# Two groups of edges in one PSUM bank, evicted together

## The chip, the cores and the metric

The kernel runs on 1 core of one Trainium2 chip. The metric is the device time of one execution in microseconds (us). Five engines run their own instruction streams and meet through semaphores: TensorE (PE; its weight loads are listed apart as PEld), VectorE (DVE), ScalarE (ACT), GpSimd (POOL) and SyncE (SP), which issues most DMAs. PE writes its results to PSUM, which has eight banks; each bank holds 512 float32 columns in each of 128 partitions.

## The reference

Two layers of a graph network on N = 1250 nodes with 1024 features and 41250 edges (`src`, `dst`, sorted by `dst`, each with one of two relations). Cut to what matters here:

```python
h = relu(layernorm(x))
# layer 0: relational convolution, D_FF = 286
norm_x = ln_weight * h * rsqrt(mean(h*h) + 1e-6)
out = norm_x @ W_root + bias
for r in range(2):
    w = (edge_type == r)
    sums = segment_sum((norm_x[src] @ W_rel[r]) * w[:, None], dst)
    out = out + sums / max(segment_sum(w, dst), 1)[:, None]
x = x + h + elu(out) @ wo
# layer 1: graph attention over the same edges
g = relu(layernorm(x)) @ W
e = exp(-leaky_relu(al[src] + ar[dst], 0.1))
x = x + elu(segment_sum(e * g[dst], src) / (segment_sum(e, src) + 1e-5))
```

## The kernel before

Both layers use a dense matrix of counts: how many edges of relation r go from node s to node d. The kernel keeps it in SBUF as the tile `cnt` in fp16. Its rows (the partitions) are the source nodes modulo 128; its columns are 20 blocks (10 source tiles times 2 relations) of 1280 destination nodes. With it the segment sums become matrix products: `means(t)` (L800) multiplies `cnt` with the rows `y`, ten destination tiles one after the other, and starts once all of `cnt` is there.

The change is in the first stage, which builds `cnt` while it computes the products of layer 0. It takes the first 190 us or so. Its two strands are these.

**The products.** For each of 10 node tiles t there are 16 steps, each a matmul of 429 columns in float32 at L723 (eight slices of the 1024 features, two halves). Around them stand, for tiles ahead and behind, by a fixed table (`plan`, `first_plan`, `late_plan`): the row statistics (DVE) and `rstd` (ACT, L550), `norm`, which makes `h` (ACT, L560), `square`, which makes the mean square and `rms` (ACT, L566 and L568), `turn(t, g)`, four PE transposes of `h` into a bank `tp` (L578), `scaled(t, g)`, four ACT copies out of that bank into `hT` (L585), and the three parts that turn the product into `y` (DVE L593, L599, L610, L616; ACT L603, L612). `residual` (POOL, L589) issues the DMA that adds `h` to `x`. `count_over` (DVE, L656 to L661, once, in tile 2) looks for edges that the fast way can't hold.

**The counts.** The edges stand in 162 groups (NG) of 256; a group is two chunks (J) of 128 edges, one edge to a partition. All edges of a group have destinations within W = 12 columns of the group's first one. For each chunk DVE compares a number of the edge with a counter and so makes a one-hot row of 2 x 10 x 12 = 240 columns, `key` (L522; five buffers). For two groups at a time it makes the one-hot rows of the source nodes, `lo` (L495; two buffers). PE multiplies the two (L523), which adds up the counts of the group in 240 columns of a PSUM bank. After the first chunk of a group a matmul of 20 columns (L526) adds what the last chunk before it left over for this group's first column. When the second chunk is in, ACT reads the group's first destination from SBUF into a register (L528) and copies the 240 sums to their place in `cnt` at that offset (L530): 20 blocks of 12 columns. Windows of neighbouring groups overlap, and the later group's copy is the valid one, so the copies must land in the order of the groups.

`chunks()` is a generator, and the loop over the steps draws from it after each L723 matmul about two chunks, spread evenly over the 160 steps. The order on PE, DVE and ACT is the written order of the program; nothing is reordered by a scheduler.

The banks: two pairs hold the products (`mm`). The other four hold the counts and the transposes. `bank(name)` takes one of three, the one freed longest, and `own_bank(name)` a fourth; groups with q % 4 == 3 take the fourth, and the other groups, the two transpose tiles of each node tile and a small one (`turn_worst`) share the three. A matmul that opens a bank waits until ACT has read what was in it.

The lines of a group, as they stand:

```python
acc = (own_bank if q % 4 == 3 else bank)("acc").rearrange("p a b -> p (a b)")
a3 = acc[:, :2 * T * W].rearrange("p (c w) -> p c w", w=W)
...
if j == J - 1:
    b = nc.values_load(first[0:1, q:q + 1], engines=[mybir.EngineType.Activation], ...)
    nc.scalar.activation(cnt_w[:, :, bass.ds(b, W)], a3, AF.Copy)
```

Of the kernel before, what the change touches and what calls it, by code (L numbers as in the profile page):

```python
# [13 lines left out]
AF = mybir.ActivationFunctionType  # L14
# [12 lines left out]
N = 1250  # L27
T = 10
ROWS = [min(128, N - t * 128) for t in range(T)]
PE_ = 128  # L30
J = 2
GE = J * PE_
NG = 162
W = 12
# [376 lines left out]
def fast_arm(tc, ctx, edges, firsts, w_root, conv_bias, wo, w_gat, a_gat, out,  # L411
# [4 lines left out]
    nc = tc.nc  # L416
# [7 lines left out]
    cnt_w = cnt_raw.rearrange("p (c n) -> p c n", n=NPAD)  # L424
# [47 lines left out]
    with ExitStack() as c1:  # L472
# [5 lines left out]
        first = firsts_at[:PE_]  # L478

        idle = own_bank("idle")  # L480
        for _ in range(12):
# [8 lines left out]
            engines={mybir.EngineType.PE, mybir.EngineType.DVE, mybir.EngineType.Activation}))  # L490
        los = {}

        def low_hots(q):
            los[q // 2] = hot.tile([PE_, 128, 2 * J], BF16, name="lo", bufs=2)
            nc.vector.tensor_tensor(  # L495
                los[q // 2], iota_lo,
                lows[:, q:q + 2, :].rearrange("p q j -> p (q j)")[:, None, :].to_broadcast([PE_, 128, 2 * J]),
                ALU.is_equal,
            )

        def carry_hots(q, q1):
            nc.vector.tensor_tensor(hot_ck[:, q:q1], iota_ck[:, None, :].to_broadcast([PE_, q1 - q, 2 * T]),
                                    ck[:, q:q1, None].to_broadcast([PE_, q1 - q, 2 * T]), ALU.is_equal)
# [3 lines left out]
        def chunks():  # L507

            for q in range(NG):
                if q % 2 == 0 and q // 2 not in los:  # L510
                    low_hots(q)
                if q in CARRIES:
                    carry_hots(q, CARRIES[q])
                acc = (own_bank if q % 4 == 3 else bank)("acc").rearrange("p a b -> p (a b)")
                a3 = acc[:, :2 * T * W].rearrange("p (c w) -> p c w", w=W)
                if q:

                    last = los[(q - 1) // 2][:, :, ((q - 1) % 2) * J + J - 1]
                    carry = (a3[:, :, 0:1], last, hot_ck[:, q - 1, :, None])
                for j in range(J):  # L520
                    key = hot.tile([PE_, 2 * T * W], BF16, name="key")
                    nc.vector.tensor_scalar(key, iota_key, keys[:, q, j:j + 1], None, op0=ALU.is_equal)  # L522
                    nc.tensor.matmul(acc[:, :2 * T * W], los[q // 2][:, :, (q % 2) * J + j], key, start=(j == 0),  # L523
                                     stop=(j == J - 1))
                    if q and j == 0:
                        nc.tensor.matmul(*carry, start=False, stop=False)  # L526
                    if j == J - 1:
                        b = nc.values_load(first[0:1, q:q + 1], engines=[mybir.EngineType.Activation],  # L528
                                           min_val=0, max_val=N - 1)
                        nc.scalar.activation(cnt_w[:, :, bass.ds(b, W)], a3, AF.Copy)  # L530
                    yield

        chunk = chunks()

        def some(n):
# [170 lines left out]
        for t in range(T):  # L706
            pys[t] = ps.tile([128, 2, 512], F32, name="mm")
            for i in range(SK):
# [12 lines left out]
                if (t, i) in late_plan:  # L721
                    late_plan[t, i]()
                nc.tensor.matmul(pys[t][:ROWS[t], r, :F + HF], hTs[t][0][:, k, :ROWS[t]], wcat[k][:, r, :],  # L723
                                 start=(k == 0), stop=(k == KD - 1))
# [492 lines left out]
    with tc.manual_schedule(  # L1217
            engines={mybir.EngineType.PE, mybir.EngineType.DVE, mybir.EngineType.Activation}):
# [84 lines left out]
    with tc.manual_schedule(  # L1303
            engines={mybir.EngineType.PE, mybir.EngineType.DVE, mybir.EngineType.Activation,
                     mybir.EngineType.Pool}):
# [264 lines left out]
```

## Time and profile before

| what | before |
|---|---|
| median of 3 executions (lowest to highest) | 593.46 us (593.29 to 594.02) |
| the profiled execution: its time, its span | 593.43 us, 591.6 us |
| PE busy | 571.1 us (97% of the span) |
| DVE busy | 412.0 us (70%) |
| ACT busy | 284.2 us (48%) |
| granted clock of PE, mean | 0.996 |

The span goes from the first to the last instruction. A matmul's end is modelled from how matmuls follow each other in the pipeline, so "busy" includes some overlap; what counts is when the next one starts. In the list of waits a line reads: engine, tile and line that waited, after the arrow what it waited for, then the total in us, how often, and the longest. In the timeline a line reads: start in us, duration, engine, line, operation, output<-inputs, shapes, count, and in brackets the idle time of the engine before it and what ended it. In the busy time by stretches the columns are the busy us of PE, PEld, DVE, ACT and POOL with the number of instructions, the granted clock of PE as a share of full speed, the share of DMA time and GB/s.

### The profile page before, as it was taken

To read this page: it belongs to the slowest core of one execution; us is meant where nothing else is said; L and a number is where in the kernel's file an instruction comes from. 1 tells how busy PE (TensorE), PEld (TensorE's weight loads), DVE (VectorE), ACT (ScalarE), POOL (GpSimd) and SP (SyncE) were. 2 spreads that over 40 slices of the span, in tenths; PEclk is the share of its full clock that TensorE was granted. 3 is DMA by queue.
4 is the path that set the end of the run, shared out by engine and by line. 5 is a ranking of instruction groups with operands and counts; after the bars stand their busy time and mean duration, and the time that the engine had idled before them with its cause. 6 is when DMAs were issued, how large, how long until landed. Compare 5 with 4: busy or idle time off the path is not lost. (4 is left out here: it accounts for less than half of the span.)

```text
span 591.6 us, 8893 instructions
## 1 busy us (share of the span) xinstructions
PE 571.1 (97%) x2894; PEld 412.1 (70%) x2894; DVE 412.0 (70%) x1051; ACT 284.2 (48%) x694; POOL 25.6 (4%) x41
## 2 busy tenths in 40 slices
PE   7899999999999999999999999999999999999994
PEld 5555555655555776776766788888888778888872
DVE  5788787887774666658899926141749988887732
ACT  3676666756663000002332124253727488877722
POOL 4010000000000000000000000000033000000000
PEclk9999999999999999999999999999999999999998
DMA  8951111011105800010015730000010122222211
GB/s 280 342 138 19 37 37 37 13 24 36 29 2 212 248 37 37 35 72 37 37 71 166 209 98 0 2 0 1 0 37 2 37 101 78 75 94 81 86 67 50
DMA packets 21933, 43.85 MB, mean 74 GB/s; under 512 B 2511, under 2 KB 7887, under 8 KB 21877
## 3 DMA queue, kind: packets, MB, share of 16 engines
q1 hardware_dynamic: 20308, 38.07, 18.7%
q0 software_dynamic: 1424, 5.12, 4.6%
q8 instruction: 24, 0.39, 0.3%
q14 instruction: 33, 0.26, 0.2%
q10 hardware_dynamic: 144, 0.00, 0.0%
HBM read 24.55 MB, written 13.52 MB: 64 GB/s over the span
## 5 line engine op out<-in xcount | busy, mean ns | idle before, releaser
L723 PE MATMUL mm<-w,hT 128*128 128x429 f32 (+1 forms) x320 | 145.8, 542 | 1.7 <-DMA w<-in_w_cat_dram 1.7
L530 ACT ACTIVATE cnt<-acc 128x240 f32 x162 | 63.5, 392 | 61.0 <-PE acc L523 38.5
L522 DVE TENSOR_SCALAR key<-meta 128x240 bf16<-128x240 f16 x324 | 74.9, 277 | 4.6 <-PE acc L523 1.8
L800 PE MATMUL mm<-y,cnt 128*128 128x286 bf16 (+3 forms) x600 | 75.2, 285 | 0.3 <-DVE y L616 0.3
L800 PEld LDWEIGHTS <-cnt 128*128 128x128 f16 (+1 forms) x600 | 59.5, 99 | 14.7 <-issue 1.0
L523 PEld LDWEIGHTS <-lo 128*128 128x128 bf16 x324 | 35.7, 114 | 44.4 <-issue 23.7
L523 PE MATMUL acc<-key,lo 128*128 128x240 bf16 x324 | 61.6, 268 | 4.7 <-ACT cnt L530 3.9
L723 PEld LDWEIGHTS mm<-w,hT 128*128 128x128 f32 (+1 forms) x320 | 48.8, 190 | 6.2 <-issue 3.7
L495 DVE TENSOR_TENSOR lo<-meta 128x512 bf16<-128x512 f16 x81 | 34.1, 421 | 26.0 <-PE acc L526 25.1
L991 PE MATMUL mm<-w,a 128*128 128x257 f32 (+3 forms) x192 | 44.5, 379 | 0.0
L811 ACT ACTIVATE bias<-bias 128x286 f32<-128x286 f32 (+1 forms) x10 | 4.4, 442 | 80.2 <-DVE bias L810 80.2
L991 PEld LDWEIGHTS mm<-w,a 128*128 128x128 f32 (+1 forms) x192 | 35.7, 187 | 5.5 <-ACT h L1017 0.2
L846 PE MATMUL mm<-wo,meta 128*128 128x512 f32 (+1 forms) x80 | 37.6, 592 | 0.0
L526 PEld LDWEIGHTS <-lo 128*128 128x128 bf16 x161 | 18.3, 114 | 24.1 <-issue 24.0
L1099 ACT ACTIVATE d<-meta,score 128x128 f32<-128x128 f32 x84 | 27.2, 389 | 10.0 <-DVE d L1116 10.0
L1161 PE MATMUL tp<-hm,zm 128*128 128x512 f32 (+1 forms) x120 | 30.1, 400 | 0.6 <-ACT tp L1167 0.6
L526 PE MATMUL acc<-meta,lo 128*128 128x20 bf16 x161 | 29.4, 183 | 0.0
L1099 ACT ACTIVATE d<-meta,tenths 128x128 f32<-128x128 f32 x84 | 27.2, 389 | 0.0
L1161 PEld LDWEIGHTS tp<-hm,zm 128*128 128x128 f32 (+1 forms) x120 | 21.6, 184 | 6.0 <-ACT tp L1167 0.6
L1161 PE MATMUL tp<-hh,zh 128*128 128x512 f32 (+3 forms) x60 | 23.7, 396 | 0.0
L1161 PE MATMUL tp<-parts,zl 128*128 128x512 f32 (+3 forms) x60 | 23.7, 395 | 0.0
L1161 PE MATMUL tp<-hh,parts 128*128 128x512 f32 (+1 forms) x60 | 23.6, 394 | 0.0
(207 smaller groups left out, 1010.3 us busy)
## 6 DMA issues: line engine op xcount, KB each, us to landing
x<-h POOLq DMA_DIRECT2D x9, 512.0 KB, 5.1
xd<-x SPq DMA_DIRECT2D x9, 512.0 KB, 2.6
x<-in_x_dram SPq DMA_DIRECT2D x8, 512.0 KB, 12.8
w<-in_L_gnn_W_dram SPq DMA_DIRECT2D x8, 512.0 KB, 7.5
w<-in_w_cat_dram SPq DMA_DIRECT2D x8, 429.0 KB, 10.1
squares<-cnt SPq DMA_DIRECT2D x10, 320.0 KB, 3.4
d<-squares SPq DMA_DIRECT2D x40, 80.0 KB, 2.1
d<-xd SPq DMA_DIRECT2D x9, 256.0 KB, 2.8
```

The lines of the kernel that those rows point to most:

```text
L495: nc.vector.tensor_tensor(los[q // 2], iota_lo, lows[:, q:q + 2, :].rearrange("p q j -> p (q j)")[:, None, :].to_broadcast([PE_, 128, 2 * J]),
L522: nc.vector.tensor_scalar(key, iota_key, keys[:, q, j:j + 1], None, op0=ALU.is_equal)
L523: nc.tensor.matmul(acc[:, :2 * T * W], los[q // 2][:, :, (q % 2) * J + j], key, start=(j == 0), stop=(j == J - 1))
L526: nc.tensor.matmul(*carry, start=False, stop=False)
L530: nc.scalar.activation(cnt_w[:, :, bass.ds(b, W)], a3, AF.Copy)
L723: nc.tensor.matmul(pys[t][:ROWS[t], r, :F + HF], hTs[t][0][:, k, :ROWS[t]], wcat[k][:, r, :], start=(k == 0), stop=(k == KD - 1))
L800: nc.tensor.matmul(pm[:n, r, :f], cnt[:k, h, r, t * 128:t * 128 + n], ybs[h][:k, s, r, :f], start=(h == 0 and s == 0), stop=(h == T - 1 an ...
L811: nc.scalar.activation(ex[:n], ex[:n], AF.Exp)
L846: nc.tensor.matmul(po[:n, c, :], oT[:, i, :n], wo_of[i][:, cs], start=(i == 0), stop=False)
L991: nc.tensor.matmul(o[:a.shape[2], :c1 - c0], a[:, k, :], b[k][:, c0:c1], start=(start and k == 0), stop=(k == KH - 1), skip_group_check=no ...
L1099: nc.scalar.activation(form[:, t - t0, :], rows[:, s, :], AF.Exp, bias=n[:, t:t + 1], scale=scale)
L1161: nc.tensor.matmul(sums_of[s, c][:n], at(sets[s % 2][f], t, t + 1)[:k, 0, :n], h[:k, c * HD:c * HD + HD], start=(t == 0 and f == "h"), sto ...
```

## The change

Group q and group q+1 (q even) now share one bank: the first takes its columns 0 to 239, the second 240 to 479. A bank is taken for each even group; every fourth pair (q % 8 == 6) takes the fourth bank. The copies of both groups, with their register loads, are issued behind the second matmul of the odd group, first the even one's, then the odd one's. There are as many matmuls, keys, register loads and copies as before, of the same sizes.

```diff
-                acc = (own_bank if q % 4 == 3 else bank)("acc").rearrange("p a b -> p (a b)")
-                a3 = acc[:, :2 * T * W].rearrange("p (c w) -> p c w", w=W)
+
+                if q % 2 == 0:
+                    both = (own_bank if q % 8 == 6 else bank)("acc").rearrange("p a b -> p (a b)")
+                acc = both[:, q % 2 * 2 * T * W:(q % 2 + 1) * 2 * T * W]
+                a3s = acc.rearrange("p (c w) -> p c w", w=W)
+                reads = [(q, a3s)] if q % 2 == 0 else [reads[0], (q, a3s)]
                 if q:
 
                     last = los[(q - 1) // 2][:, :, ((q - 1) % 2) * J + J - 1]
-                    carry = (a3[:, :, 0:1], last, hot_ck[:, q - 1, :, None])
+                    carry = (a3s[:, :, 0:1], last, hot_ck[:, q - 1, :, None])
                 for j in range(J):
                     key = hot.tile([PE_, 2 * T * W], BF16, name="key")
                     nc.vector.tensor_scalar(key, iota_key, keys[:, q, j:j + 1], None, op0=ALU.is_equal)
-                    nc.tensor.matmul(acc[:, :2 * T * W], los[q // 2][:, :, (q % 2) * J + j], key, start=(j == 0),
+                    nc.tensor.matmul(acc, los[q // 2][:, :, (q % 2) * J + j], key, start=(j == 0),
                                      stop=(j == J - 1))
                     if q and j == 0:
                         nc.tensor.matmul(*carry, start=False, stop=False)
-                    if j == J - 1:
-                        b = nc.values_load(first[0:1, q:q + 1], engines=[mybir.EngineType.Activation],
-                                           min_val=0, max_val=N - 1)
-                        nc.scalar.activation(cnt_w[:, :, bass.ds(b, W)], a3, AF.Copy)
+                    if j == J - 1 and len(reads) == 2:
+                        for g, a3 in reads:
+                            b = nc.values_load(first[0:1, g:g + 1], engines=[mybir.EngineType.Activation],
+                                               min_val=0, max_val=N - 1)
+                            nc.scalar.activation(cnt_w[:, :, bass.ds(b, W)], a3, AF.Copy)
                     yield
```

## The prediction

> **What bounds the kernel now.** I first read the busy time by stretches, to see where PE is not full.
>
> ```profile
> 80.00:100.00 20.00, 19.42 (x104) 11.53 (x103) 15.44 (x60) 13.10 (x38) 1.53 (x3) 1.00 0.14 27
> 200.00:220.00 20.00, 20.00 (x144) 14.68 (x142) 14.18 (x34) 0.89 (x2) 0.00 (x0) 1.00 0.27 83
> ```
>
> Behind the count stage (200 us on) PE is busy for all 20 us of each stretch; in it, some 0.6 us of 20 are lost at full granted clock. ACT has room (13.1 of 20). Whatever PE loses in this stage moves the whole rest, which PE bounds. So next the list of waits, PE's alone:
>
> ```profile
> PE acc L523 <- ACT cnt L530: 3.9, 5, 1.1
> PE mm L723 <- DMA w<-in_w_cat_dram: 1.7, 2, 1.1
> ...
> PE tp L578 <- ACT hT L585: 1.2, 2, 0.6
> PE acc L523 <- ACT hT L585: 0.8, 1, 0.8
> ...
> PE tp L578 <- ACT cnt L530: 0.3, 1, 0.3
> ```
>
> Four of these are one cause: PE opens a PSUM bank whose last contents ACT has not copied out yet, counts (L530) or transposes (L585). That makes 6.2 us; the weights' DMA is early (10.9 and 18.9 us) and not touched. How such a wait looks, in the timelines of PE and of ACT:
>
> ```profile
> 65.12 0.27 PE L523 MATMUL acc<-key,lo 128*128 128x240 bf16 x1
> 66.52 0.27 PE L523 MATMUL acc<-key,lo 128*128 128x240 bf16 x1 [1.12 <-ACT cnt L530]
> 66.62 0.18 PE L526 MATMUL acc<-meta,lo 128*128 128x20 bf16 x1
> ```
>
> ```profile
> 65.37 0.29 ACT L568 ACTIVATE rms<-ssq,eps 128x1 f32<-128x1 f32 x1
> 66.03 0.44 ACT L530 ACTIVATE cnt<-acc 128x240 f32 x1 [0.37 <-issue]
> 66.75 0.44 ACT L530 ACTIVATE cnt<-acc 128x240 f32 x1 [0.29 <-ACT cnt L530]
> 67.47 0.44 ACT L530 ACTIVATE cnt<-acc 128x240 f32 x1 [0.28 <-ACT cnt L530]
> ```
>
> ACT was held up by `sq` and `rms`, copies at 66.03 to 66.47, and PE starts at 66.52. From start to start that step took 1.40 us; where PE doesn't wait it takes 0.10 to 0.11, so the loss is 1.29, more than the idle 1.12 that the bracket shows, as ends are modelled. I summed the losses so, start to start against the median of like steps: 22.7 us 0.23, 25.8 0.94, 38.3 0.57, 42.9 0.06, 45.6 0.64, 47.7 1.07, 61.1 0.14, 66.5 1.29, 94.6 0.73, 103.0 1.00, 130.7 0.73, 138.9 0.71, 156.4 0.21, 164.0 0.26. Together **8.6 us**, all of them waits for a bank. The last two ACT rows show the other price that I need: copies that follow each other come every 0.72 us (the register load on ACT's queue stands between), or about 0.46 where ACT was busy with something long and the load ran ahead (60.63 and 61.09).
>
> **The change, part by part.**
>
> *Banks.* PE and DVE keep the same instructions in the same order, and PE's matmuls have the same sizes: nothing there (loads of weights and keys as before). A bank is now taken per two groups. A group takes some 1.04 us of PE (67.56, 68.59, 69.63, 70.67), so with four banks a bank comes up again after about 8 groups, 8.3 us, instead of 4.2: 4.1 us more. It is held longer by one group and by the second copy, 1.04 + 0.72 = 1.8 us. Net, PE should come about 2.3 us later than ACT's release compared to now. I checked it wait by wait: for each matmul that opens a bank in the changed program I looked up what it waits for, and took both times from this trace. Now there are 157 such waits; in the median PE comes 1.5 us after ACT's instruction has ended, 12 of them under 0.1 us (PE waited), 25 under 0.7. With the new banks there are 81; median 3.5 us, one under 0.1, four under 0.7. The wait at 66.5 is gone altogether (that group is the second of its pair), and the next opening, at 67.56, has 5.0 us to spare, 3.7 once PE comes 1.29 sooner.
>
> *The copies.* As many as before (162 by 392 ns), with as many register loads. Even ones move behind the odd group's second matmul. So what stands behind a pair on ACT (L550, L560, L566, L568, L585, L603, L612) starts up to 0.72 us later wherever ACT had been waiting for PE; where ACT was behind, nothing changes. Who waits for those: PE for L585 and L560, DVE for L550, L568, L603, L612, POOL for `h` (its DMA lands 5 us after the issue and is needed a tile of 17 us later). ACT does wait for PE often (38.5 us in 56 places), so the delay is real; what counts is whether somebody is there. DVE in this stage waits mostly for PE, and for ACT two times, 0.7 us each. PE's openings behind L585 with under 0.72 us to spare are few: at 77.6 us (0.50 us) and 113.8 (0.29), so at worst (0.72 − 0.50) + (0.72 − 0.29) = 0.65; I take 0.53, by a delay of 0.66. SP's and POOL's queues keep their order.
>
> *What is left of the 8.6.* Four places. At 25.8 us the bank still holds transposes; with the 0.94 + 0.23 before it gone PE arrives at the next opening at 26.81 − 1.17 = 25.64, ACT's last `hT` copy ends at 25.79: 0.15. At 38.3 the transposes need the pair of groups 18 and 19, whose copies now follow each other behind `y` (37.30, then 0.30 to 0.46 later): 0.2. At 130.7:
>
> ```profile
> 129.09 0.38 ACT L530 ACTIVATE cnt<-acc 128x240 f32 x1 [0.53 <-PE acc L523]
> 129.35 0.28 ACT L550 ACTIVATE rstd<-mv,eps 128x1 f32<-128x1 f32 x1
> 129.54 1.13 ACT L585 ACTIVATE hT<-tp,lnw 128x128 f32<-128x128 f32 x4
> ```
>
> ```profile
> 129.97 0.18 PE L526 MATMUL acc<-meta,lo 128*128 128x20 bf16 x1
> 130.72 0.66 PE L578 MATMUL tp<-ident,h 128*128 128x128 f32 x4 [0.57 <-ACT hT L585]
> ```
>
> The transposes wait for four `hT` copies that stand behind a group's copy. In the changed program they need the pair 106 and 107 instead: the first copy starts at 129.09, the second 0.66 later and ends at 130.12; PE would be there at 129.99, so 0.16 with the 0.05 of the signal. At 94.6 the copies of `hT` now stand ahead of group 72's copy (92.95) instead of behind it, and the wait is gone. Fourth, what was covered: at 45 to 47 us DVE does `count_over`, and its next key ends at 47.18. Without 0.64 + 1.07 PE is there at 48.67 − 1.71 = 46.96: about 0.3 us, DVE being late next. DVE's keys already cost PE 0.4 us (31.2, 52.8, 79.8, 91.2); with PE closer behind I add as much again.
>
> *The end of the stage.* The last pair's second copy ends at about 184.1 instead of 183.4; `means` reads `cnt` from 187 us on, covered by the last L723 matmuls; 0.7 if they were not there.
>
> Sum: 8.56 − (0.15 + 0.2 + 0.16 + 0.3 + 0.53 + 0.4 = 1.74) = 6.8 us. Against the profiled execution: 593.43 − 6.8 = **586.6 us** (its median stands at 593.46, the same within 0.03).
>
> **The rivals.** *The waits only move* (the burst is paid widely): ACT's delay of 0.7 us behind pairs reaches PE at half of the 18 sets of `hT` copies from tile 1 on: 6.3 us, leaving a gain of 2.3: 591.2 us. For it: ACT waits for PE at 56 places, and a `hT` copy ended four of the waits above. Against it: only two openings have less than 0.7 us to spare.
>
> *Keys.* DVE is busy for 15 to 17 us of 20 in this stage; if it, not ACT, is the next bound, a gain ends where PE has caught up. Its keys are ready 1.17 us ahead in the median, but under 0.6 us in 25 of 324 cases; if those each cost 0.15 us, the gain is 8.56 − 3.75 − 1.34 (the other terms) = 3.5: 590.0. Against it: DVE itself waits 25.1 us for PE to free `lo`, so it follows PE.
>
> *The bank becomes scarcer* (slower): the copy is late by a group, and transposes do not keep the groups' rhythm. If the 18 sets of transposes from tile 1 on found the pair just copied and each waited 0.7 us for its second copy, that is 12.6 us against 8.6 removed: 597.4. It decides once more than 12 of the 18 wait so. Against it: by the banks of the changed program one does (130.7). The Trainium skill, "PSUM — Partial Sum Buffer", section "Summary: rules for kernel authors", speaks against the change in this sense: evacuate promptly, as PSUM is tight; and it has PE and the reader use different banks, which is why the even group's copy must wait at all. By that rule the time would come out as this rival's. This trace does not bear it out: ACT's spare time is the longer one by the 2.3 us above.
>
> *No change:* some later wait takes up the gain, for instance the DMAs of the next stage's weights, which start when the products end. They would have to end last, but PE is full from 200 us on, and the list shows no wait for them. 593.4.
>
> **How the numbers follow.** About 0.2% (1.2 us) is what a measurement of this kernel tells from no change. Forecast 0.64 (584.9 to 589), waits that move or keys 0.21 (589 to 592.2), no change 0.05, scarcer banks or another loss 0.10. So faster 0.85, same 0.05, slower 0.10. Range: from all 8.6 us gained with nothing left, 584.9, to the weakest of the partial cases, 591.2.
>
> **What would show it.** Right: PE's waits for ACT in the first 190 us fall from 6.2 us to under 1.5; none of the long ones at `rms`; ACT's waits at L530's successor come half as often and are longer; the second copy of each pair follows the first by about 0.7 us; means starts some 7 us earlier and the rest of the trace keeps its length. Wrong: PE waits for `hT` or `h` in many places (the burst), PE's weight loads and matmuls wait for `key` (DVE), or the first stage shortens and a later stage grows.

## The result, and the profile after

| | before | changed |
|---|---|---|
| median (lowest to highest), 4 runs each on one chip | 593.59 us (593.29 to 594.02) | 587.16 us (587.08 to 587.84) |
| ratio, 95% interval | | 0.9894 [0.9877, 0.9911] |
| profiled execution: time, span | 593.43, 591.6 us | 587.84, 586.0 us |
| start of the last matmul of the products (L723, now L728) | 186.73 us | 181.18 us |
| from there to the end of the span | 404.9 us | 404.9 us |

The changed kernel is 6.4 us faster. The whole difference lies in the first stage; behind it nothing changed length. From L523 on the lines have moved by 4 or 5: the chunk's matmul is L527, the small one L530, the register load L533, the copy L535, transposes L583, `hT` copies L590.

The busy time by stretches, changed kernel (busy us of PE, PEld, DVE, ACT, POOL; granted clock; DMA):

```profile
80.00:100.00 20.00, 20.00 (x108) 11.96 (x107) 16.04 (x61) 13.43 (x37) 1.28 (x3) 1.00 0.24 46
200.00:220.00 20.00, 20.00 (x122) 13.41 (x121) 13.88 (x34) 0.89 (x2) 0.00 (x0) 1.00 0.07 27
```

The stretch that had 19.42 us of PE is now full. PE's waits, in the order of their totals:

```profile
PE mm L728 <- DMA w<-in_w_cat_dram: 2.7, 2, 2.0
...
PE acc L527 <- ACT hT L590: 1.1, 2, 0.8
```

Of the four kinds of waits for a bank one stands there still, with 1.1 us in two places. The weights' DMA, which the change doesn't touch, is 1.0 us longer than in the profile of before. ACT's own waits from 14 to 190 us, before and then after:

```profile
ACT cnt L530 <- PE acc L523: 38.5, 56, 5.2
ACT cnt L530 <- ACT cnt L530: 10.7, 33, 0.8
```

```profile
ACT cnt L535 <- PE acc L527: 25.2, 32, 7.2
ACT cnt L535 <- ACT cnt L535: 22.3, 74, 0.9
```

By this list ACT waited for PE 38.5 us in 56 places and now does 25.2 us in 32; copy behind copy went from 33 to 74 places. So the copies do come in pairs. The name PE is not right everywhere: in 37 of the 56 places, and in 19 of the 32, the last matmul that the copy needs had ended more than 0.35 us before the copy started, and ACT waited for its own register load. The place of the 1.29 us loss, PE's and then ACT's timeline:

```profile
63.77 0.27 PE L527 MATMUL acc<-key,lo 128*128 128x240 bf16 x1
63.87 0.18 PE L530 MATMUL acc<-meta,lo 128*128 128x20 bf16 x1
63.90 0.38 PE L527 MATMUL acc<-key,lo 128*128 128x240 bf16 x2
```

```profile
63.40 0.29 ACT L573 ACTIVATE rms<-ssq,eps 128x1 f32<-128x1 f32 x1
64.66 0.44 ACT L535 ACTIVATE cnt<-acc 128x240 f32 x1 [0.97 <-PE acc L527]
65.32 0.44 ACT L535 ACTIVATE cnt<-acc 128x240 f32 x1 [0.23 <-ACT cnt L535]
```

The last row of PE merges two matmuls; the second of them, at 64.01 us, is the one that stood at 66.52 before, and it no longer waits. The 0.97 us that ACT stands idle behind `rms` are put down to PE by the bracket, but the last matmul of that pair had ended at 61.3 us. It is the register load, which started at 63.40 and took 0.88 us; PE now has the room to go on meanwhile. The second copy follows the first after 0.66 us.

By the prediction's method (start to start, against the median of like steps) PE's losses to banks fell from 8.6 to 1.9 us: 0.99 at 27.4 us, 0.26 at 38.6, 0.47 at 75.6, 0.18 at 126.4. Losses to late keys rose from 0.37 to 0.73, those to the weights' DMA from 2.1 to 3.1. That is −6.7 + 0.35 + 1.0 = −5.35 us; the last L728 starts 5.55 us sooner, and the two profiled executions are 5.59 us apart. The other three executions of the changed kernel took 587.08 to 587.21.

### The profile page after: what moved, and what is told of

It reads as the page before. It is cut to its first block, busy times and chain, and to the rows that moved or that the text cites. A ratio compares the mean times of both kernels' runs of the same rounds, so it can differ in the third digit from the quotient of the medians.

```text
span 586.0 us, 8877 instructions
## 1 busy us (share of the span) xinstructions
PE 569.8 (97%) x2894; PEld 412.3 (70%) x2894; DVE 411.1 (70%) x1051; ACT 286.7 (49%) x694; POOL 26.3 (4%) x41
## 5 line engine op out<-in xcount | busy, mean ns | idle before, releaser
L728 PE MATMUL mm<-w,hT 128*128 128x429 f32 (+1 forms) x320 | 145.8, 542 | 2.7 <-DMA w<-in_w_cat_dram 2.7
L535 ACT ACTIVATE cnt<-acc 128x240 f32 x162 | 63.5, 392 | 53.7 <-PE acc L527 25.2
L527 PEld LDWEIGHTS <-lo 128*128 128x128 bf16 x324 | 35.7, 113 | 45.3 <-issue 30.6
L527 PE MATMUL acc<-key,lo 128*128 128x240 bf16 x324 | 61.0, 268 | 1.2 <-ACT hT L590 1.1
L728 PEld LDWEIGHTS mm<-w,hT 128*128 128x128 f32 (+1 forms) x320 | 48.7, 189 | 7.2 <-issue 6.4
L530 PEld LDWEIGHTS <-lo 128*128 128x128 bf16 x161 | 18.3, 114 | 19.0 <-issue 18.7
L530 PE MATMUL acc<-meta,lo 128*128 128x20 bf16 x161 | 29.4, 183 | 0.0
```

The source lines that it names most:

```text
L527: nc.tensor.matmul(acc, los[q // 2][:, :, (q % 2) * J + j], key, start=(j == 0), stop=(j == J - 1))
```

## The experiments

The theory: the gain comes from the time until a bank is opened again, which doubles. Rivals: it comes from the copies (they stand elsewhere on ACT's queue, in pairs), or from one bad place that happened to move. Besides the times, I summed PE's losses from 10 to 197 us in each profile (every start that comes over 0.03 us late, against the medians of both kernels), by what the profile names as the releaser:

| kernel | profiled us | banks (ACT) | keys, `lo` (DVE) | weights (DMA) | time less losses |
|---|---|---|---|---|---|
| before | 593.43 | 8.5 | 0.9 | 2.0 | 582.0 |
| changed | 587.84 | 2.0 | 1.1 | 3.0 | 581.7 |
| changed, again | 587.10 | 1.8 | 1.0 | 2.7 | 581.6 |
| copies in pairs only | 593.48 | 8.6 | 0.8 | 2.1 | 582.0 |
| pairs, three banks | 590.39 | 5.6 | 0.75 | 2.3 | 581.7 |
| before, three banks | 601.50 | 15.2 | 1.3 | 2.7 | 582.3 |
| both loads first | 597.88 | 8.6 | 5.4 | 2.0 | 581.9 |
| before, add on POOL | 597.91 | 2.1 | 10.4 | 1.4 | 584.0 |
| eight keys | 586.71 | 1.5 | 1.25 | 2.4 | 581.6 |
| loads first, eight keys | 596.80 | 7.65 | 4.75 | 2.2 | 582.2 |

In all but one the time less the losses is the same within 0.7 us: what PE loses in this stage decides the time. (The DVE column holds a wait of `means` for `y` too, 0.5 us in before and after.)

**The copies alone.** The kernel before, a bank for each group, but both copies behind the odd group:

```diff
-                if q % 2 == 0:
-                    both = (own_bank if q % 8 == 6 else bank)("acc").rearrange("p a b -> p (a b)")
-                acc = both[:, q % 2 * 2 * T * W:(q % 2 + 1) * 2 * T * W]
+                acc = (own_bank if q % 4 == 3 else bank)("acc").rearrange("p a b -> p (a b)")[:, :2 * T * W]
```

(against the changed kernel)

> The copies of two groups stand behind the odd group's second matmul, as in the changed kernel, but each group has a bank of its own, as in the kernel before. Theory (banks): the gain is the longer time until a bank comes up again; here that stays at four groups (4.2 us) while each even group holds its bank for some 1.8 us longer, so nothing is gained and PE waits for banks more than the 8.6 us of before: 594 to 602 us. Rival (ACT's queue): the gain comes from half as many waits of ACT for PE and from copies that follow each other; those are here too, so 587 to 589 us.

593.55 us, ratio to before 0.9993 [0.9983, 1.0002]. Its list of PE's waits (its lines are 2 above those of the changed kernel):

```profile
PE acc L525 <- ACT cnt L533: 2.7, 4, 1.1
...
PE acc L525 <- ACT hT L588: 1.6, 3, 0.6
PE tp L581 <- ACT hT L588: 1.1, 2, 0.6
PE tp L581 <- ACT cnt L533: 0.6, 1, 0.6
```

All four kinds of bank waits of before are back, with 6.0 us by the list (6.2 before). So the pairing of the copies brings nothing. It costs nothing either: I had expected 594 to 602 us, as the even group's bank is held a group longer. But it hardly is: in the median the even group's copy ends 1.4 us behind that group's second matmul in place of 1.2 before, the odd one's 1.0 in place of 1.1. ACT was mostly behind by about a group already.

**Fewer banks.** The same comparison with the fourth bank left empty, once for pairs, once for single groups:

```diff
-                    both = (own_bank if q % 8 == 6 else bank)("acc").rearrange("p a b -> p (a b)")
+                    both = bank("acc").rearrange("p a b -> p (a b)")
```

> The changed kernel with three banks for counts and transposes instead of four (the fourth stands empty). Theory (banks): a bank comes up after six groups, 6.2 us, instead of 8.3; that is 2.1 us more than before, of which the longer hold takes 1.8: most of the gain is gone, 590 to 594 us, with PE's waits for ACT back at 4 to 8 us. Rival (ACT's queue): 587 us, as ACT's instructions are the same.

```diff
-                acc = (own_bank if q % 4 == 3 else bank)("acc").rearrange("p a b -> p (a b)")
+                acc = bank("acc").rearrange("p a b -> p (a b)")
```

> The kernel before with three banks instead of four for counts and transposes: a bank comes up after 3.1 us instead of 4.2. Theory (banks): the openings lose 1.0 us of their room (median 1.5), so a third to a half of the 157 waits bite: 605 to 625 us. Rival (ACT's queue): ACT's instructions are those of before, so about 593 us, at most a few us more.

Pairs on three banks: 590.79 us, ratio 0.9949 [0.9932, 0.9965]. Single groups on three: 601.95 us, 1.014 [1.012, 1.016], less than I had expected. PE's longest waits for banks from 14 to 190 us, the pairs first, then the single groups:

```profile
PE acc L527 <- ACT cnt L535: 2.2, 4, 0.8
PE tp L583 <- ACT cnt L535: 1.1, 3, 0.6
```

```profile
PE acc L523 <- ACT cnt L530: 8.9, 11, 1.6
PE tp L578 <- ACT hT L585: 2.1, 4, 0.6
PE tp L578 <- ACT cnt L530: 1.0, 1, 1.0
```

The four versions lie in order of the time until a bank is opened again (banks times groups in each times the 1.04 us of a group, transposes aside): 3.1 us 601.95, 4.2 us 593.97 (before, on the same chip), 6.2 us 590.79, 8.3 us 587.16 (the result above). The first step gives 8.0 us for 1.04 us more, the other two 3.2 and 3.6 us for 2.08 us each; that fewer of ACT's delays outlast a longer time is the likely reason, but it was not counted. Three shared banks beat four single ones. This is what the theory says and neither rival does. One thing this series doesn't part: from single groups to pairs the times that PE opens a bank also fall, from 183 to 102 in the stage, and on three banks a pair finds its bank free no earlier than a single group did on four (0.9 and 1.1 us before PE comes, in the median). So the 3.2 us of the middle step may be for the fewer openings as much as for the longer time. The other two steps keep the number of openings and show the time alone.

**What makes the copies late.** The big losses before follow a pattern. ACT's queue at the place of the 1.29 us: the register load at 62.62 us took 0.86 us in place of 0.28, so the copy behind it started at 63.91; `sq` and `rms` stood next, and the following load and copy could only start at 65.38 and 66.03. Ten of the stage's register loads took over 0.7 us, and every one of them lies between the issue and the landing of a `residual` DMA (this one 61.0 to 66.1). The loads of the kernel before (shortest/median/longest ns):

```profile
L528 ACTq TENSOR_LOAD <-meta x162: 270/276/1188, 9.7 to 182.1; - x162
```

To see whether that DMA slows them, the addition goes to POOL itself:

```diff
-            nc.gpsimd.dma_start(xs[t][:n], hs_.pop(t)[:n], accum_op=ALU.add)
+            nc.gpsimd.tensor_add(xs[t][:n], xs[t][:n], hs_.pop(t)[:n])
```

> The kernel before, with x + h added by an instruction of POOL instead of by an accumulating DMA (residual). In the trace of before ACT's register loads (L528, 0.28 us) take 0.4 to 1.2 us in the 5 us in which that DMA runs, and the long waits of PE stand behind them. Theory: the DMA slows the loads; without it they stay at 0.28 and the waits at 45.6, 66.5, 103.0 and 138.9 us shrink by some 0.6 each: 590.5 to 591.5 us unless POOL's add slows DVE. Rival: the loads are slow for another reason (they stand behind a blocked queue), stay at 0.9, and the time stays at 593 us or grows.

598.06 us, ratio 1.0072 [1.0055, 1.0088], not the 590.5 to 591.5 us of the theory, which held only if POOL's addition did not slow DVE. The loads of that kernel:

```profile
L528 ACTq TENSOR_LOAD <-meta x162: 271/275/481, 9.8 to 184.9; - x162
```

With the DMA the longest takes 1188 ns, without it none is over 481. That the DMA slows the loads is shown. The losses to banks fell to 2.1 us, but this can't be put down to the loads alone, as PE came later for another reason. POOL's and DVE's timelines:

```profile
62.06 2.35 POOL L589 TENSOR_TENSOR x<-x,h 128x1024 f32<-128x1024 f32 x1 [8.23 <-ACT h L560]
```

```profile
62.69 2.02 DVE L495 TENSOR_TENSOR lo<-meta 128x512 bf16<-128x512 f16 x1 [0.75 <-PE acc L526]
```

`lo`, 0.42 us elsewhere, takes 2.02 and ends 0.3 us behind POOL's addition; a key that meets such an addition takes up to 2.51 us in place of 0.28. The Trainium skill, "SBUF — State Buffer", section "Who interferes with whom", says that a DVE instruction with two SBUF inputs contends with a GpSimd instruction that reads SBUF; the 2.02 us agree. Some 2 us of that kernel's time lie outside the losses counted (584.0 in the table). Of these 1.6 lie behind DVE's last instruction, where the span runs on for 7.8 us in place of 6.2, so not in this stage; why is open. So the DMA is the cheaper of the two, and the sharing of banks makes nearly all its slow loads harmless: in the changed kernel they go on (0.88 us at 63.4 us), and from 39 us on no wait of PE for a bank follows one within 11 us. No kernel was run that has neither the DMA nor POOL's addition.

**Both loads ahead of both copies.** If the 0.66 us of a pair were of weight, loading both offsets first should shorten it:

```diff
-                        for g, a3 in reads:
-                            b = nc.values_load(first[0:1, g:g + 1], ...)
+                        places = [nc.values_load(first[0:1, g:g + 1], ...) for g, _ in reads]
+                        for b, (_, a3) in zip(places, reads):
                             nc.scalar.activation(cnt_w[:, :, bass.ds(b, W)], a3, AF.Copy)
```

> The changed kernel with both register loads of a pair ahead of its first copy, so that the second copy follows the first by about 0.45 us (its own length and a signal) instead of 0.67. Theory (what is left at banks is the length of the pair's burst on ACT): the four places lose up to 0.2 us each less, 586.3 to 587.0 us. Rival (the burst costs nothing; what is left comes from hT and sq): the same time as the changed kernel, within 0.3 us; a little more where the two loads stand behind rms and the first copy comes later.

598.35 us, ratio to before 1.0075 [1.0062, 1.0088]: 11 us slower than the changed kernel, where I had expected a little less than it. ACT's timeline:

```profile
105.86 0.78 ACT L535 ACTIVATE cnt<-acc 128x240 f32 x2 [1.65 <-PE acc L530]
107.54 0.77 ACT L535 ACTIVATE cnt<-acc 128x240 f32 x2 [0.91 <-PE acc L530]
109.23 0.77 ACT L535 ACTIVATE cnt<-acc 128x240 f32 x2 [0.92 <-PE acc L530]
```

The two copies do stand 0.40 us apart, but where ACT is behind, the pairs come every 1.69 us. In the changed kernel copies that follow each other start 0.66 us apart in a pair and 0.72 us between pairs, so a pair costs 1.38. The loads show why. In the changed kernel a load between such copies starts 0.014 us after a copy has started and runs beside it. With both loads first, the second copy waits at the head of ACT's queue until the first has ended (105.86 and 106.26 us), and only then do the next pair's loads start, at 106.27 and 106.84, with nothing beside the second; the copy follows at 107.54. The bracket names PE, but the pairs follow faster than the 2.08 us that PE takes for one, so PE doesn't set this pace; the two loads do. ACT has then 2.08 − 1.69 = 0.39 us in each pair's time for its other work, where the changed kernel leaves it 0.70. By the stretch from 80 to 100 us that work is about 0.6 us (13.43 busy, less 19 copies of 0.392, is 6.0 in 20 us); this sum is an estimate, as it leaves out what runs beside the loads. ACT does fall behind: the even group's copy ends 3.6 us behind that group's second matmul in the median, 2.2 in the changed kernel. And the losses are back: 8.6 us to banks, 5.4 to DVE.

**More keys, and the changed kernel once more.** The one cost that DVE puts into the changed kernel is keys; eight buffers in place of five let DVE run ahead:

```diff
-                    key = hot.tile([PE_, 2 * T * W], BF16, name="key")
+                    key = hot.tile([PE_, 2 * T * W], BF16, name="key", bufs=8)
```

> The changed kernel with 8 buffers for key instead of 5, so that DVE can run further ahead. Theory (PE's waits for key, 0.7 us, are buffers that come free too late): 586.4 to 586.9 us. Rival (DVE is late because of its own long work just before, count_over and the parts of y, and lo's two buffers bound how far it runs ahead): the same as the changed kernel within 0.3 us.

> The changed kernel itself, on the chip of the three kernels beside it. Every theory: 587 to 588 us; in its profile, PE's losses to banks at about 27, 38, 75 and 126 us again, some 1.9 us in all, and DVE's keys some 0.7 us.

586.75 us, ratio to before 0.9885 [0.987, 0.9899], beside 587.52 us (587.10 to 589.82), 0.9908 [0.9891, 0.9924], for the changed kernel. The loss behind `count_over` fell from 0.24 to 0.05 us, but the sum for DVE did not fall (1.0 to 1.25). It is the lowest time of all, but the intervals overlap: the two aren't told apart.

With both edits, loads first and eight keys:

> Both edits of the two kernels beside it. If both theories hold, 585.8 to 586.6 us; if both rivals hold, the changed kernel's time within 0.3 us.

598.28 us, ratio 1.0074 [1.0061, 1.0087]. More keys bring nothing measurable to the version with both loads first (DVE's losses 4.75 in place of 5.4 us), so those are mostly not for want of buffers; what makes DVE late there was not separated.

## Why the prediction came out right, and where its sizes were off

The forecast was 586.6 us, the median is 587.16. Point by point:

- *The bound.* Right: PE's losses in the first stage are the time, and nothing behind it took up the gain (404.9 us in both). The "no change" rival falls.
- *The banks.* The mechanism is right, as the copies alone and the three-bank versions show. The size of the room, the time for which a bank has been free when PE comes, was not: "median 3.5 us, one under 0.1, four under 0.7" of 81 openings. Counted over all 98 openings of a bank that was used before, each taking the bank that was released first, the old trace's times give 3.2 us, one and four; measured are 2.4 us, six and eleven. For the kernel before the same count gives 1.1 us, 19 and 60 of 179, where the forecast read 1.5 us, 12 and 25 of 157: the room was smaller than it read. The forecast took ACT's release times from the old trace and left PE's as they were, but PE has moved ahead by what it no longer loses, and a pair's release comes with its second copy.
- *25.8 us, the term that was mis-sized most: 0.15 forecast, 0.99 measured (now at 27.4).* ACT's timeline there, then PE's:

```profile
22.92 0.38 ACT L535 ACTIVATE cnt<-acc 128x240 f32 x1 [0.36 <-PE tp L583]
23.60 0.37 ACT L535 ACTIVATE cnt<-acc 128x240 f32 x1 [0.30 <-ACT cnt L535]
24.76 0.44 ACT L535 ACTIVATE cnt<-acc 128x240 f32 x1 [0.79 <-PE acc L530]
25.92 0.44 ACT L535 ACTIVATE cnt<-acc 128x240 f32 x1 [0.71 <-ACT cnt L535]
26.21 1.13 ACT L590 ACTIVATE hT<-tp,lnw 128x128 f32<-128x128 f32 x4
```

```profile
27.39 0.26 PE L527 MATMUL acc<-key,lo 128*128 128x240 bf16 x1 [0.83 <-ACT hT L590]
```

  The `hT` copies stand behind two pairs that come 0.7 to 1.2 us apart, not 0.66: the register loads at 23.6 and 24.8 us took 0.72 and 0.44 us, and behind the second another 0.3 us passed before its value was used, all inside the residual DMA of 21.5 to 30.9 us. The working had priced the transposes' bank by the old end of `hT` (25.79) and saw neither the burst in front of it nor the slow loads.
- *38.3 us:* 0.2 forecast, 0.26 measured. *130.7 us:* 0.16 and 0.18 (now 126.4).
- *The burst at 77.6 and 113.8 us:* 0.53 together; 0.47 measured, all of it at one place (75.6). The sum is right, the split isn't.
- *Count_over:* 0.3 and 0.24. *Keys:* 0.4 more forecast; without `count_over` they cost 0.49 after and 0.37 before, so 0.1 more. DVE together: 0.7 forecast, 0.35 measured.
- Bank terms came to 1.9 in place of 1.04, DVE to 0.35 in place of 0.7, and the weights' DMA, set at nothing, cost 1.0 more in the profiled execution: 6.8 − 0.86 + 0.35 − 1.0 = 5.3 us, where the two profiled executions are 5.6 us apart. Without the DMA's term it is 6.3, near the 6.4 us of the medians; the other executions have no profile, so what the DMA cost them is not known. Why that DMA's wait differs between the profiles (1.4 to 3.0 us over all of them) stays open.
- *The copies.* "ACT does wait for PE often (38.5 us in 56 places)" took the brackets at their word; in two thirds of these places ACT waited for its own load. What the forecast needed of it, that a later copy seldom meets a waiting PE, came out all the same.
- *Waits that only move, keys, scarcer banks* fall with these numbers. Against the first: PE's waits for `hT` are two, not nine. Against the second: late keys cost 0.7 us in all, not 3.75. Against the third: one set of transposes waits for a pair's second copy at 126.4, one at 38.6, not twelve. The rule of the Trainium skill that stood behind it ("PSUM — Partial Sum Buffer", "Summary: rules for kernel authors": evacuate promptly) does not decide here: in the changed kernel the two copies of a pair end 2.2 and 1.9 us behind their group's second matmul in the median, in place of 1.2 and 1.1, and it is 6.4 us faster.
- *The signs.* PE's waits for ACT under 1.5 us: 1.1 in the list. ACT's waits for PE fewer and the longest longer: 56 to 32, 5.2 to 7.2 us. Second copy about 0.7 us behind: 0.66. `means` some 7 us earlier: 5.55, in the execution with the longer DMA wait.

## What to carry to other kernels

A buffer that PE waits for now and then, while the reader has time to spare on average, can be helped by a longer return time with the reader no faster: compute for each opening when the last contents were released and when the writer comes, and share a bank if its columns allow, even at the price of a later release. Do this sum with the writer moved ahead by what it gains, and with the reader's queue as it will then stand. Do not hoist a register load past a copy that waits: what stands behind a waiting instruction on its queue, the next loads among them, waits too.

## What the runs showed of the hardware that was not expected

- A register load on ACT's queue, 0.28 us in the median, took 0.7 to 1.3 us at times while an accumulating DMA issued by POOL was under way, and never over 0.48 us in the kernel without these DMAs.
- A load behind a copy on ACT's queue starts 0.014 us after the copy does and is in part hidden by it: copies start 0.66 to 0.72 us apart with a load between, 0.40 without. Two loads in a row ahead of both copies are hidden less: 1.69 us a pair in place of 1.38, and 11 us in the kernel's time.
- A POOL addition of 128 x 1024 float32 (2.35 us) holds a `lo` or a key of DVE that meets it until it ends: 2.02 us in place of 0.42 for `lo`, up to 2.51 in place of 0.28 for a key.
